# Attention output divided by its weight sums before it is turned, with values and sums in one stretch

## The chip, the cores and the metric

The kernel runs on one core of a Trainium2 chip. A core has a matrix engine (TensorE, PE in the profile; its weight loads are shown as PEld), a vector engine (VectorE, DVE), a scalar engine (ScalarE, ACT), a general engine (GpSimd, POOL) and a queue for transfers (SyncE, SP). Each engine works through its own list of instructions in the order of the program and waits where a semaphore of another engine is not there yet. Matmuls write to PSUM, which VectorE and ScalarE can read[...].

The metric is the device time of one execution in microseconds (us), smaller being better. Three runs of the kernel before took 3242.97, 3245.24 and 3245.39 us, so the median is 3245.24 us.

## The reference, cut to what matters

There are 32 batches (B) of 224 rows (S) with 512 features (D), and a context of 750 rows with 384 features per batch. Attention has 16 heads of 32 features. A head's output is the weighted sum of the values divided by the sum of the weights, which is what `softmax` followed by the product with `v` means:

```
attn = jnp.einsum('bhnd,bhmd->bhnm', q * scale, k)
attn = jnp.where(pad_mask[:, None, :, None], attn, jnp.float32(-1000000000.0))
attn = jax.nn.softmax(attn, axis=-1)
out  = jnp.einsum('bhnm,bhmd->bhnd', attn, v)
...
x = x + jnp.tanh(g_xattn[0]) * _L0_xattn_ref(_layernorm(x, axis=-1), ctx_768, ...)
x = x + jnp.tanh(g_ffn[0]) * _L0_ffn_ref(_layernorm(x, axis=-1), ...)
```

The second line of `x` is a feed-forward layer (512 to 2048 to 512) with quantised weights and activations, over all 7168 rows. The gate of the attention is multiplied into the value weights once at the start.

## The kernel before, in words

**Steps.** The attention is cut into 128 steps, one for each batch `b` and group `g` of four heads (128 features). A main loop (line 802) runs over the steps. The heads of a step share the 128 partitions of the matrix array, 32 rows or 32 columns each.

**What a step does.** The scores are computed twice. `maxima` (line 276) computes them with queries on the partitions (tile `sm`) in three parts, and VectorE takes the largest of each row (`mx`, 2.24 us a part). `minus_max` turns the maximum into three bfloat16 parts. `weights` (line 333) computes the scores again with context rows on the partitions (tile `se`), the maximum subtracted by an extra matmul from `nT`, and ScalarE takes `Exp` into the tile `p`, in three parts `u`. GpSimd adds the parts up into `acc`, which holds for each query the weights still to be summed over 125 partitions. `values` (line 366) multiplies the weights with the values into the PSUM tile `po`, features on the partitions and queries along the row. `sums` (line 380) multiplies `acc` with ones into the second half of the same tile, so that each feature's row has its weight sum beside it, and ScalarE copies both halves to the tile `oT`. `finish` (line 392) turns both halves with four transposes into `pyt`, queries on the partitions; VectorE takes the reciprocal of one column per head (`rd`), multiplies (`yo`), and GpSimd adds `yo` into `x`. After the fourth group of a batch the rows of `x` are stored to memory, from where the feed-forward layer loads them.

**Slots.** Step n of the main loop has six slots, 0 to 5. The even slots hold one part of `maxima` for step n+1, the odd slots one part of `weights` for step n. All of these use the one tile of the pool `ps_s` (four banks of PSUM, one buffer). So `sm`, its reduction on VectorE, `se`, its `Exp` on ScalarE and the next `sm` take turns, and TensorE has time between them for other matmuls, which I call the **cover** of the slot: in an even slot it covers the reduction, in an odd slot the `Exp`.

**What the covers are.** They are put in by hand with `put(slot, us, function)`. For step n−1 (called `last`), `values` goes to slot 1, `sums` to slot 3 and `finish` to slot 4. For later steps there are the keys (`pk`, one half in slot 0 and the other in slot 2), the queries (`pq`), the values (`pv`) and the turning of the normalised `x` (`pxn`). The turning of the maximum (`pn`) is in slot 0. Units marked `first=True` come directly behind the scores of the slot, then pieces of the feed-forward layer, then the other units:

```
            used = sum(us for us, _ in slots[k])
            early = [unit for us, unit in slots[k] if unit in quick]
            for unit in early:
                unit()
            ...
                ffn.fill(
                    (PE_ROOM[k % 2] - used, (1.1, 2.2)[k % 2], 1.7),
                    B if n == N and k > 4 else (n - 1) // NG if n else 0,
                )
```

**The planner.** `ffn.fill` takes pieces of the feed-forward layer (`ph`, `po` from `w2q`, the transposes `phq` and `pxq`, and their VectorE, ScalarE and GpSimd work) as long as they fit a room of microseconds per engine. The room of TensorE is 2.7 us in even and 2.2 us in odd slots, less what the units of the slot say they use. The numbers in `put` therefore move pieces between slots. While the weights of the feed-forward layer are being quantised (the first twelve steps) there are no such pieces. What is left when the steps are done follows behind them.

**Buffers.** The small PSUM tiles (`po`, `pyt`, `pk`, `pq`, `pv`, `ph` and so on) share the four buffers of the pool `ps_m`. Each engine's instructions keep the order in which the program issues them.

Of the kernel before, what the change touches and what calls it, by code (L numbers as in the profile page):

```python
# [8 lines left out]
F32 = mybir.dt.float32  # L9
# [5 lines left out]
ALU = mybir.AluOpType  # L15
# [9 lines left out]
def flamingo_gated_layer(  # L25
# [27 lines left out]
    pe, dve, act = Ordered(nc.tensor), Ordered(nc.vector), Ordered(nc.scalar)  # L53
    gp = Ordered(nc.gpsimd)
    P = 128
    B, S, D = x.shape
# [3 lines left out]
    NQ = 2  # L60
    CP = S // NQ
    H, DH = 16, 32
    HG = P // DH
# [13 lines left out]
    ident = const.tile([P, P], F32, name="ident")  # L77
# [53 lines left out]
    def pool(name, bufs, space=None):  # L131
        kw = {} if space is None else {"space": space}
        return es.enter_context(tc.tile_pool(name=name, bufs=bufs, **kw))
# [10 lines left out]
    smp = pool("small", 2)  # L144
# [6 lines left out]
    ps_m = pool("ps_m", 4, PSUM)  # L151
# [12 lines left out]
    x_of, y_of, q_of, k_of, v_of = {}, {}, {}, {}, {}  # L164
# [4 lines left out]
    def load_y(b):  # L169
        y_of[b] = yp.tile([P, NYC, M], F32, tag="y", name=f"y_{b}")  # L170
        nc.sync.dma_start(y_of[b], ctxT[b].rearrange("(c p) m -> p c m", p=P))

    def load_x(b):
        x_of[b] = xp.tile([CP, NQ, D], F32, tag="x", name=f"x_{b}")
        nc.sync.dma_start(x_of[b], x[b].rearrange("(t p) d -> p t d", p=CP))
# [52 lines left out]
    def k_units(b, g):  # L228
        kT = kp.tile([P, M], F32, tag="kT", name=f"kT_{b}_{g}")
        k_of[b, g] = kT  # L230

        def piece(half):
            pk = ps_m.tile([P, 512], F32, tag="m", name=f"pk_{b}_{g}_{half}")
            for c in range(NYC):
                pe.matmul(
                    pk[:, :MH], wkv_sb[:, c, g * P : (g + 1) * P],
                    y_of[b][:, c, half * MH : (half + 1) * MH],
                    start=(c == 0), stop=(c == NYC - 1),
                )
            act.copy(kT[:, half * MH : (half + 1) * MH], pk[:, :MH])  # L240

        return [lambda h=h: piece(h) for h in range(2)]
# [79 lines left out]
    def turn_max(n):  # L322
        b, g = steps[n]
        pn = ps_m.tile([P, NQ, CP], BF16, tag="m", name=f"pn_{b}_{g}")
        for t in range(NQ):
            pe.transpose(
                pn[:, t, :], nbs[n % 2][:, t].rearrange("p j r -> p (j r)"), identb[:CP, :CP]
            )
        nT = smp.tile([P, S], BF16, tag="nT", name=f"nT_{b}_{g}")
        act.copy(nT, pn.rearrange("p t n -> p (t n)"))  # L330
        nT_of[b, g] = nT
# [34 lines left out]
    def values(b, g):  # L366

        po = ps_m.tile([P, 512], F32, tag="m", name=f"po_{b}_{g}")
        po_of[b, g] = po
        v = v_of[b, g // 2]  # L370
        for c in range(NKC):
            for j in range(HG):
                at = ((g % 2) * HG + j) * DH
                pe.matmul(
                    po[j * DH : (j + 1) * DH, :S], v[:, c, at : at + DH],
                    p_of[b, g, c // 2][:, j, c % 2, :],
                    start=(c == 0), stop=(c == NKC - 1),
                )

    def sums(b, g):  # L380

        po, acc = po_of[b, g], acc_of.pop((b, g))
        for j in range(HG):
            pe.matmul(
                po[j * DH : (j + 1) * DH, S : 2 * S], ones[:KC, :DH], acc[:, j, :],
                start=True, stop=True,
            )
        oT = smp.tile([P, 2 * S], F32, tag="oT", name=f"oT_{b}_{g}")
        act.copy(oT, po[:, : 2 * S])
        po_of[b, g] = oT  # L390

    def finish(b, g):

        oT = po_of.pop((b, g))
        pyt = ps_m.tile([P, 2, NQ, P], F32, tag="m", name=f"pyt_{b}_{g}")
        for a in range(2):
            for t in range(NQ):
                at = a * S + t * CP
                pe.transpose(pyt[:CP, a, t, :], oT[:, at : at + CP], ident)
        rd = smp.tile([CP, NQ, HG], F32, tag="rd", name=f"rd_{b}_{g}")  # L400
        dve.reciprocal(
            rd, pyt[:CP, 1].rearrange("p t (j d) -> p t j d", j=HG)[:, :, :, 0]
        )
        yo = smp.tile([CP, NQ, P], F32, tag="yo", name=f"yo_{b}_{g}")
        dve.tensor_tensor(
            yo.rearrange("p t (j d) -> p t j d", j=HG),
            pyt[:CP, 0].rearrange("p t (j d) -> p t j d", j=HG),
            rd.unsqueeze(3).to_broadcast([CP, NQ, HG, DH]),
            ALU.mult,
        )  # L410
        cols = slice(g * P, (g + 1) * P)
        gp.tensor_tensor(x_of[b][:, :, cols], x_of[b][:, :, cols], yo, ALU.add)
        if g == NG - 1:
            nc.sync.dma_start(
                x1_d[b * S : (b + 1) * S, :].rearrange("(t p) d -> p t d", p=CP), x_of[b]
            )
# [361 lines left out]
    ks = k_units(0, 0) + k_units(0, 1)  # L778
# [23 lines left out]
    for n in range(N + 1):  # L802
        b, g = steps[n] if n < N else (B, 0)
        nxt = steps[n + 1] if n + 1 < N else None
        last = steps[n - 1] if 0 < n else None
        slots = [[] for _ in range(6)]
        quick = []

        def put(k, us, fn, first=False):
            slots[k].append((us, fn))  # L810
            if first:
                quick.append(fn)

        if n < N:
            put(0, 0.2, lambda: turn_max(n), first=True)
        if last:
            put(1, 2.3, lambda: values(*last), first=True)
            put(3, 0.5, lambda: sums(*last), first=True)
            put(4, 0.5, lambda: finish(*last), first=True)
        if n + 2 < N:  # L820
            ks = k_units(*steps[n + 2])
            put(0, 1.9, ks[0])
            put(2, 1.9, ks[1])
        if n < N and g == 2 and b + 2 < B:
            put(0, 0.0, lambda: (load_y(b + 2), load_x(b + 2)))
        more = b + 1 < B and n < N
        if more and g == 0:
            norm, turns, qs = q_units(b + 1)
            put(0, 0.0, norm[0], first=True)
            put(2, 0.0, norm[1], first=True)  # L830
            put(4, 0.0, norm[2], first=True)
            put(5, 2.7, lambda: v_piece(b + 1, 0, 0))
        if n < N and g < 2:
            put(3, 1.4, lambda: v_piece(b, 1, g + 1, 0))
            put(4, 1.4, lambda: v_piece(b, 1, g + 1, 1))
        if more and g == 1:
            put(0, 0.25, turns[0])
            put(2, 0.25, turns[1])
            put(5, 2.7, lambda: v_piece(b + 1, 0, 1))
        if more and g == 2:  # L840
            put(3, 1.5, qs[0])
            put(4, 1.5, qs[1])
            put(5, 2.7, lambda: v_piece(b + 1, 0, 2))
        if more and g == 3:
            put(3, 1.5, qs[2])
            put(4, 1.5, qs[3])
            put(5, 2.7, lambda: v_piece(b + 1, 1, 0))
        for k in range(6):
            if k % 2 == 0:
                if nxt:  # L850
                    maxima(*nxt, k // 2)
            elif n < N:
                weights(b, g, k // 2)
            if k == 4 and nxt:
                minus_max(n + 1)
# [5 lines that stand above are left out]
            if wunits:  # L861
                if k in (1, 3, 5):
                    wunits.pop(0)()
            else:
# [4 lines that stand above are left out]
            for us, unit in slots[k]:  # L869
                if unit not in quick:  # L870
                    unit()
# [39 lines left out]
```

## Time and profile before

| | us | instructions |
|---|---|---|
| median of three runs | 3245.24 | |
| profiled execution | 3241.06 | |
| its span | 3239.3 | 65769 |
| TensorE busy (matmuls) | 3060.1 | 28642 |
| VectorE busy | 1712.6 | 2501 |
| ScalarE busy | 1647.5 | 1803 |
| GpSimd busy | 2069.2 | 3048 |
| four transposes per step `pyt` | 83.5 | 512 |
| copy `oT` on ScalarE | 67.5 | 128 |
| `rd` and `yo` on VectorE | 25.3 and 54.3 | 128 and 128 |
| addition into `x` on GpSimd | 100.6 | 128 |

The span reaches from the first to the last instruction of the program, and 1.8 us of the profiled execution lie outside of it. The busy time of matmuls is longer than what they occupy, because their ends are modelled and they overlap; the distance from the start of one group of matmuls to the start of the next is what a group costs. Nearly all instructions are recorded by a helper and so have the line 51; they are told apart by the tiles they write and read. A step takes 25.3 us on average (3239.3 divided by 128).

### The profile page before, as it was taken

Reading aid. Unit: us, or ns where it says so; the run is one execution under the profiler, and the core shown is the slowest. Engines: PE = TensorE matmul, PEld = TensorE weight load, DVE = VectorE, ACT = ScalarE, POOL = GpSimd, SP = SyncE. Lnnn points to the kernel's source line nnn. Section 1 sums busy time; section 2 is a strip of 40 time slices with the busy share of each in tenths; the row PEclk is TensorE's granted clock in tenths of the full one; section 3 lists DMA queues with packets and bytes.
Section 4 is the critical chain, followed back from the end, with each engine's and each line's share of the span. In section 5 each row is a group of like instructions: output and inputs, shape, how many; then the busy total and the mean of one; then the engine's idle time right before and its main releaser. Section 6 shows DMA issues by size and latency. Waiting matters only on the chain. (4 is left out here: it accounts for less than half of the span.)

```text
span 3239.3 us, 65769 instructions
## 1 busy us (share of the span) xinstructions
PE 3060.1 (94%) x28642; PEld 1976.6 (61%) x28642; DVE 1712.6 (53%) x2501; ACT 1647.5 (51%) x1803; POOL 2069.2 (64%) x3048
## 2 busy tenths in 40 slices
PE   7989999999999999999999999999999999999975
PEld 5655566666666666666666666666666666666643
DVE  4576555554465455555554554555555545545533
ACT  2333555555555455455555554555455455555554
POOL 2565667666666676667666666765676666667664
PEclk9999999999999999999999999999999999999988
DMA  3322111010101001101000111001100011110000
GB/s 134 103 75 65 33 40 40 16 39 26 40 30 36 26 25 33 37 32 40 20 29 30 40 36 39 27 16 40 40 30 26 26 33 37 36 40 20 4 20 29
DMA packets 52817, 120.51 MB, mean 37 GB/s; under 512 B 3888, under 2 KB 3888, under 8 KB 52400
## 3 DMA queue, kind: packets, MB, share of 16 engines
q1 hardware_dynamic: 52528, 116.32, 11.0%
q8 instruction: 223, 3.65, 0.5%
q14 instruction: 66, 0.54, 0.1%
HBM read 86.94 MB, written 29.36 MB: 36 GB/s over the span
## 5 line engine op out<-in xcount | busy, mean ns | idle before, releaser
L51 POOL TENSOR_TENSOR acc<-acc,p 125x896 f32<-125x896 f32 x512 | 1069.4, 2089 | 518.3 <-ACT p L51 497.4
L51 DVE TENSOR_REDUCE mx<-sm 112x4 f32<-112x2000 f32 (+1 forms) x384 | 860.9, 2242 | 986.6 <-PE sm L51 986.6
L51 ACT ACTIVATE p<-se 125x1792 f32<-125x1792 f32 x384 | 638.8, 1664 | 413.1 <-PE se L51 407.1
L51 PE MATMUL pk<-y,wkv_sb 128*128 128x375 f32 x1536 | 537.8, 486 | 15.8 <-DMA wkv_sb<-in_wkvT 12.1
L51 PE MATMUL sm<-kT,qT 32*112 32x500 f32 (+1 forms) x4096 | 426.8, 508 | 35.2 <-ACT p L51 34.7
L51 POOL TENSOR_TENSOR acc<-p 125x896 f32<-125x896 f32 x128 | 267.3, 2089 | 273.0 <-ACT p L51 272.9
L51 ACT COPY kT<-pk 128x375 f32<-128x375 f32 x256 | 120.8, 472 | 581.9 <-PE pk L51 581.3
L51 PEld LDWEIGHTS pk<-y,wkv_sb 128*128 128x128 f32 x1536 | 278.6, 190 | 172.2 <-issue 26.7
L51 PE MATMUL pv_None<-wkv_sb,y 128*125 128x256 f32 x1536 | 364.1, 387 | 0.0
L51 PE MATMUL se<-qT,kT 32*125 32x224 f32 x6144 | 362.7, 349 | 0.0
L51 PE MATMUL po<-p,v 125*32 125x224 f32 x6144 | 321.4, 358 | 0.1
L51 PEld LDWEIGHTS pv_None<-wkv_sb,y 128*125 128x125 f32 x1536 | 278.4, 187 | 69.8 <-issue 33.4
L51 PEld LDWEIGHTS se<-qT,kT 32*125 32x125 f32 x6144 | 297.8, 183 | 0.0
L51 DVE SCALAR_TENSOR_TENSOR h<-ph,qa_am,b_sb 128x512 f32<-128x512 f32 x224 | 163.5, 744 | 197.2 <-PE ph L51 196.1
L51 PEld LDWEIGHTS sm<-kT,qT 32*112 32x112 f32 x4096 | 159.2, 170 | 166.8 <-issue 94.4
L51 PEld LDWEIGHTS po<-p,v 125*32 125x32 f32 x6144 | 188.1, 111 | 115.1 <-issue 40.1
L51 PE MATMUL ph<-w1q,xT 128*128 128x512 fp8e4 x896 | 226.8, 385 | 26.2 <-ACT xT L51 24.0
L51 PE MATMUL po<-w2q,hT 128*128 128x256 fp8e4 x1792 | 221.3, 279 | 13.1 <-DVE xg L51 7.1
L51 PE MATMUL pq<-xnT,wq_sb 128*128 128x224 f32 x1024 | 218.2, 356 | 0.2 <-ACT xnT L51 0.2
L51 PE MATMUL se<-nT,ones 3*125 3x448 bf16 x1536 | 157.2, 396 | 54.2 <-DVE mx L51 45.4
L51 POOL TENSOR_TENSOR x<-x,yo 112x256 f32<-112x256 f32 x128 | 100.6, 786 | 165.3 <-DVE yo L51 135.4
L51 PEld LDWEIGHTS <-hT 128*128 128x128 bf16 x1792 | 174.5, 100 | 48.3 <-issue 17.9
(102 smaller groups left out, 3497.3 us busy)
## 6 DMA issues: line engine op xcount, KB each, us to landing
y<-in_ctxT SPq DMA_DIRECT2D x32, 1125.0 KB, 5.4
x<-in_x SPq DMA_DIRECT2D x32, 448.0 KB, 3.9
x_d<-x SPq DMA_DIRECT2D x32, 448.0 KB, 3.1
xg<-x_d SPq DMA_DIRECT2D x28, 512.0 KB, 3.7
out<-xg SPq DMA_DIRECT2D x56, 256.0 KB, 2.1
wa<-in_w1T SPq DMA_DIRECT2D x8, 512.0 KB, 4.5
wa<-in_w2T SPq DMA_DIRECT2D x8, 512.0 KB, 4.0
wb<-in_w1T SPq DMA_DIRECT2D x8, 512.0 KB, 3.8
```

Source lines behind the costliest of these rows:

```text
L51: return lambda *args, **kw: tc.keep_in_program_order(build(*args, **kw))
```

## The change

The division moves to where the features lie on the partitions. `sums` no longer copies both halves of `po`. VectorE takes the reciprocal of the whole second half (128 partitions by 224) and multiplies it with the first half, both read from PSUM, into `oT`. `finish` turns one half only, with two transposes instead of four, and VectorE adds the result from PSUM into `x`. The copy on ScalarE, the small reciprocal, the multiplication `yo` and the addition on GpSimd are gone.

In the main loop `values` and `sums` stand one behind the other in slot 2, and the second half of the keys goes from slot 2 to slot 1. The units state 2.6 us and 0.3 us of TensorE instead of 2.3, 0.5 and 0.5 us, so the rooms of the planner change in slots 1 to 4.

```diff
-        oT = smp.tile([P, 2 * S], F32, tag="oT", name=f"oT_{b}_{g}")
-        act.copy(oT, po[:, : 2 * S])
+
+        oT = smp.tile([P, 2, S], F32, tag="oT", name=f"oT_{b}_{g}")
+        dve.reciprocal(oT[:, 1, :], po[:, S : 2 * S])
+        dve.tensor_tensor(oT[:, 0, :], po[:, :S], oT[:, 1, :], ALU.mult)
         po_of[b, g] = oT
 
     def finish(b, g):
 
         oT = po_of.pop((b, g))
-        pyt = ps_m.tile([P, 2, NQ, P], F32, tag="m", name=f"pyt_{b}_{g}")
-        for a in range(2):
-            for t in range(NQ):
-                at = a * S + t * CP
-                pe.transpose(pyt[:CP, a, t, :], oT[:, at : at + CP], ident)
-        rd = smp.tile([CP, NQ, HG], F32, tag="rd", name=f"rd_{b}_{g}")
-        dve.reciprocal(
-            rd, pyt[:CP, 1].rearrange("p t (j d) -> p t j d", j=HG)[:, :, :, 0]
-        )
-        yo = smp.tile([CP, NQ, P], F32, tag="yo", name=f"yo_{b}_{g}")
-        dve.tensor_tensor(
-            yo.rearrange("p t (j d) -> p t j d", j=HG),
-            pyt[:CP, 0].rearrange("p t (j d) -> p t j d", j=HG),
-            rd.unsqueeze(3).to_broadcast([CP, NQ, HG, DH]),
-            ALU.mult,
-        )
+        pyt = ps_m.tile([P, NQ, P], F32, tag="m", name=f"pyt_{b}_{g}")
+        for t in range(NQ):
+            pe.transpose(pyt[:CP, t, :], oT[:, 0, t * CP : (t + 1) * CP], ident)
         cols = slice(g * P, (g + 1) * P)
-        gp.tensor_tensor(x_of[b][:, :, cols], x_of[b][:, :, cols], yo, ALU.add)
+        dve.tensor_tensor(x_of[b][:, :, cols], pyt[:CP], x_of[b][:, :, cols], ALU.add)
...
         if last:
-            put(1, 2.3, lambda: values(*last), first=True)
-            put(3, 0.5, lambda: sums(*last), first=True)
-            put(4, 0.5, lambda: finish(*last), first=True)
+            put(2, 2.6, lambda: (values(*last), sums(*last)), first=True)
+            put(4, 0.3, lambda: finish(*last), first=True)
         if n + 2 < N:
             ks = k_units(*steps[n + 2])
             put(0, 1.9, ks[0])
-            put(2, 1.9, ks[1])
+            put(1, 1.9, ks[1])
```

## Prediction

> **What bounds the kernel now.** I read the page's busy times, the waits, then the timeline of one step.
>
> ```profile
> PE 3060.1 (94%) x28642; PEld 1976.6 (61%) x28642; DVE 1712.6 (53%) x2501; ACT 1647.5 (51%) x1803; POOL 2069.2 (64%) x3048
> ```
>
> TensorE is the bound: no other engine is over 64%. So an edit is worth what it takes from TensorE's list, or adds to its standstills. The waits name two of these:
>
> ```profile
> PEld sm L51 <- ACT p L51: 59.4, 63, 2.1
> ...
> PEld L51 <- DVE mx L51: 53.6, 58, 5.1
> ...
> PE se L51 <- DVE mx L51: 45.4, 120, 4.9
> ```
>
> Scores `se` wait for the reduction `mx`, scores `sm` for the `Exp` into `p`. The timeline of step 59 shows slots 2 to 4 (start, duration, engine, what, idle before):
>
> ```profile
> 1467.45 1.11 PE L51 MATMUL sm<-kT,qT 32*112 32x250 f32 x16
> ...
> 1468.49 2.16 PE L51 MATMUL pk<-y,wkv_sb 128*128 128x375 f32 x6
> ...
> 1470.92 0.41 PE L51 MATMUL se<-nT,ones 3*125 3x448 bf16 x4 [0.27 <-DVE mx L51]
> ...
> 1472.02 0.16 PEld L51 LDWEIGHTS po<-acc,ones 125*32 125x32 f32 x8 [0.28 <-issue]
> 1472.02 0.58 PE L51 MATMUL po<-acc,ones 125*32 125x224 f32 x8
> 1472.20 1.28 ACT L51 ACT_TABLE_LOAD   x1 [1.04 <-PE se L51]
> ...
> 1472.54 1.78 PE L51 MATMUL pq<-xnT,wq_sb 128*128 128x224 f32 x8
> ...
> 1475.21 1.11 PE L51 MATMUL sm<-kT,qT 32*112 32x500 f32 x8 [0.89 <-ACT p L51]
> ...
> 1476.25 0.65 PE L51 MATMUL pyt<-ident,oT 128*112 128x128 f32 x4
> ...
> 1476.74 1.68 PE L51 MATMUL pq<-xnT,wq_sb 128*128 128x224 f32 x8
> ...
> 1478.68 0.41 PE L51 MATMUL se<-nT,ones 3*125 3x448 bf16 x4 [0.27 <-DVE mx L51]
> ```
>
> Three things are to be seen. First, starts give each group's cost: `sums` 0.52 us, four transposes 0.49. From undisturbed places in the same way: half of the keys 1.98, `values` 2.41, `pq` 1.61, half a `pv` piece 1.39, `ph` 0.87, `phq` 0.45, a w2 piece 1.75. Second, from the end of `sm` to `se` an even slot takes 2.43 us however little stands between (1468.49 to 1470.92; 1476.25 to 1478.68): keys alone (1.98) lack 0.45, transposes and `pq` (2.09) lack 0.34. Third, the odd slots: from `se`'s start to `sm` with nothing between takes 2.72, of which `se` is 0.86, so the cover needed is 1.86, and about 1.92 typically. Behind a Gelu the table for `Exp` is loaded first (1.28) and 3.22 is needed; here 2.12 of cover lacks 1.1.
>
> **The Trainium skill.** "TensorEngine Tiling (Array Packing)", Key Properties, says that changing the tiling mode drains the engine. The trace agrees: every exit from the 32-wide tiles shows 0.28 of idle before the next load. "ScalarE: Activation LUTs", What ACT_TABLE_LOAD costs, gives about 1283 ns, as the trace has. "VectorE: DVE Perf Modes", tier table, puts fp32 `tensor_tensor` with a PSUM operand at one element per cycle; `yo` agrees (256 columns, 425 ns).
>
> **The change, part by part.**
>
> *Two transposes less.* The four start 0.11 apart after the first, so 2 × 0.109 = 0.22 us a step, × 128 = 27.9 us less on TensorE.
>
> *Sums behind values.* Both use 32-column tiles, so one drain goes. In `values` eight matmuls take 0.19; `sums` are two such rounds, 0.38 instead of 0.52. 0.137 × 128 = 17.5 us less. Together 45.4 us.
>
> *The covers.* I listed, from TensorE's order in both programs, what stands in each even and odd slot, and summed what it lacks against 2.43, 1.92 or 3.22:
>
> | slot | before | us | after | us |
> |---|---|---|---|---|
> | 0 | 49 × 0.34 (pn, keys) | 16.7 | 48 × 0.34 | 16.3 |
> | 1 | 17 loads × 0.81 (values) | 13.8 | 22 loads × 1.24 (keys), 3 × 0.79 | 29.7 |
> | 2 | 30 × 0.45 (keys) | 13.5 | none (values and sums 2.79) | 0 |
> | 3 | 15 loads, 0.65 to 1.31; 10 × 0.01 | 14.7 | 19 × 0.31 (pq), 13 × 0.53 (pv), 8 loads × 1.61, 2 × 0.08 | 25.9 |
> | 4 | 33 × 0.34, 11 × 0.55, 3 × 0.10 | 17.6 | 37 × 0.56, 26 × 0.77, 1 × 0.32 | 41.1 |
> | 5 | 17 loads × 0.44 | 7.5 | 17 × 0.44 | 7.5 |
> | last two steps | | 12.7 | | 14.4 |
> | sum | | 96.5 | | 134.9 |
>
> So 38.4 us of standstill are added. Half of the transposes' gain is lost where it arises, because slot 4 is short of cover already; `sums` leave slot 3 bare; only slot 2 gains. The check on before: beyond each group's shortest distance to the next, TensorE stands still 148 us up to step 125. My list explains 96, and 28 are 21 places where `ph` stands right behind `pxq` and waits for the copy to `xT` (1.27 and more each). Some 24 are left, mostly in the second step of a batch, where VectorE is late with `xn`.
>
> *The pieces shift.* The planner's new order has 15 such `pxq`–`ph` places: 6 × 1.27 = 7.6 us less. Behind the last step both orders have the same 34 groups.
>
> *VectorE.* It loses `rd` (0.20) and `yo` (0.43) and gains a product of 224 columns (`yo`'s row less 32 columns, 0.39), an addition of 256 (0.43) and a reciprocal of 128x224, which the trace doesn't show. From below: one column per cycle, 0.39. From above: the same VectorE page says, in its walkthrough of the pipeline, that the division repeats eight times; at eight cycles of 0.96 GHz per column, an estimate, 1.87 + 0.16 = 2.0. `rd` (8 columns, 198 ns against 156 for one) speaks for the lower part; I take 0.39. It hardly matters. Queued behind the two new instructions are slot 2's and 3's evictions (`h`, `xg`, `v`), `hm`, and then `mx` of slot 4, for which TensorE waits. From the end of `sums` to the end of slot 4's scores at least 3.85 us pass; VectorE's list there comes to 2.1 on average and 3.45 at most. With 2.0 for the reciprocal some six steps overflow, 2 us in all. If that cover went, each microsecond would cost 128.
>
> *ScalarE and GpSimd.* The copy `oT` (0.53) and the addition (0.79, and its waits for `yo`, 135 us) go. Neither engine is the bound: nothing, beyond an earlier `acc`. No transfer is added; the store of `x` is issued behind VectorE's addition instead of GpSimd's.
>
> *A new wait.* `sums` wait for `acc`, now in the middle of slot 2. Placing them there in the trace of before, `acc` was done at least 1.2 us earlier in all steps, 7.7 in the median. GpSimd has less to do after the change: nothing. Everything on TensorE is queued behind this wait.
>
> *The end.* In the last step `values` fall behind two w2 pieces, on the way to the last store of `x`; about 2.8 later, and 0.9 earlier by the hop over GpSimd and a hidden copy: 1 us more, an estimate.
>
> Sum: −45.4 + 38.4 − 7.6 + 1 = −13.6. On the span 3239.3 − 13.6 = 3225.7, as an execution 3241.06 − 13.6 = 3227.5. The profiled execution is 4.2 below the median of the runs, so I predict 3245.2 − 13.6 = 3231.6, rounded 3232.
>
> **Rivals.**
>
> *The gain is eaten.* The 24 unexplained microseconds grow to 38 or so, since VectorE gets more to do just before the late steps and evictions that free `ps_m` come later. For it: waits of TensorE for VectorE up to 5.1. Against: behind slot 4's `mx` VectorE's list is shorter than before (3.8 against 4.1 on average). It ends near 3245.
>
> *The gain stays whole.* GpSimd, freed of the addition, has the scales for `xn` ready earlier, so that most of the 24 go, and `po` holds a buffer for one slot instead of three. Then 3232 − 20 = 3212. For it: VectorE waited for GpSimd's `ve`, up to 4.1. Against: only three such waits.
>
> *Slower: `sums` wait for `acc`.* Place: slot 2, with nothing else to do on TensorE. In seven steps only 1.2 to 2 us were in hand, where the feed-forward layer puts up to 7 us of small work between the parts of `acc`, and the planner moves this work. The sign turns when these waits exceed 13.6 us, a result slower than noise at 20: each of the 28 pairs of row tiles would have to stop TensorE for 0.7. At 1.5 each, 42 us, it ends at 3274. Against: the longest lists between parts of `acc` are no longer than before.
>
> *It does not do what it says:* the order shows the two transposes gone and the groups adjacent in every step, so no.
>
> **How the numbers follow.** Forecast (6.5 to 22 us faster) 0.45, whole gain 0.17, eaten 0.21, slower 0.17. 0.2% or 6.5 us is about what a measurement can tell from no change. So faster 0.62, same 0.21, slower 0.17. The forecast's own range is 3223 to 3239. The range 3204 to 3256 takes in the eaten gain, the whole one with both terms' errors, and the smaller half of the waits for `acc`.
>
> **What would show it.** Right: `pyt` with 256 matmuls and some 28 us less between starts; 0.38 from `sums` to the next group less the drain; slot 4 short by 0.56 and 0.77 in about 63 steps; no wait before `se` in slot 2; waits of `sm` for `p` up by some 30 us in slots 1 and 3; VectorE busier by about 0.6 a step. Wrong: a wait of `po<-acc` for `acc`; reductions `mx` that start late after slot 4's scores; a reciprocal above 2 us; or a standstill of TensorE in slots that the table calls covered.

## The result, and the profile after

The changed kernel takes 3220.02 us (median of four runs, 3218.53 to 3220.15) beside 3245.31 us of the kernel before (four runs too). The ratio is 0.9922, with a 95% interval of 0.9909 to 0.9934. That is 25.3 us less, where the prediction had 13.6 less. The profiled execution took 3220.14 us with a span of 3218.4, which is 20.9 less than the span before.

The page of the changed kernel, busy times:

```profile
PE 3027.6 (94%) x28386; PEld 1958.6 (61%) x28386; DVE 1919.8 (60%) x2629; ACT 1580.8 (49%) x1675; POOL 1974.1 (61%) x2920
```

TensorE is the bound as before. VectorE has 207 us more to do. The groups of instructions (busy us, mean ns of one, then the idle time ahead of it) show of what:

```profile
L51 DVE RECIPROCAL oT<-po 128x224 f32<-128x224 f32 x128 | 199.3, 1557 | 76.2 <-PE po L51 76.2
L51 PE MATMUL pyt<-ident,oT 128*112 128x128 f32 x256 | 55.6, 299 | 2.2 <-DVE oT L51 2.2
L51 DVE TENSOR_TENSOR x<-pyt,x 112x256 f32<-112x256 f32 x128 | 53.0, 414 | 0.0
L51 DVE TENSOR_TENSOR oT<-po,oT 128x224 f32<-128x224 f32 x128 | 50.1, 391 | 4.4
```

The product and the addition have the forecast durations (0.39 and 0.41 against 0.39 and 0.43). The reciprocal takes 1.56 us, four times the 0.39 that I used, within the bounds of 0.39 and 2.0. The waits that answer to the three shown before:

```profile
PEld sm L51 <- ACT p L51: 115.7, 138, 3.5
...
PE se L51 <- DVE mx L51: 62.1, 115, 2.9
PEld L51 <- DVE mx L51: 51.4, 69, 1.7
```

Scores `sm` wait for `Exp` 56 us longer. By the slots, some 29 of these are in slots where ScalarE loads its table first, and most of the rest in slots 1 and 3 without a load, which lost `values` and `sums` as their cover. The waits for `mx` are up from 99.0 to 113.5 in total, but the longest fell from 5.1 to 2.9. (Each line has the total in us, the number and the longest.) No wait of `po<-acc` for `acc` is left in the list at all. Step 58 (counted from 0, one step earlier than the one in the prediction), slots 2 to 4, in the timeline of the changed kernel:

```profile
1449.85 1.11 PE L51 MATMUL sm<-kT,qT 32*112 32x250 f32 x16 [1.07 <-ACT p L51]
1450.89 2.48 PE L51 MATMUL po<-p,v 125*32 125x224 f32 x48
1453.19 0.56 PE L51 MATMUL po<-acc,ones 125*32 125x224 f32 x8
...
1454.65 0.41 PE L51 MATMUL se<-nT,ones 3*125 3x448 bf16 x4
...
1458.23 1.11 PE L51 MATMUL sm<-kT,qT 32*112 32x500 f32 x8
1459.27 0.43 PE L51 MATMUL pyt<-ident,oT 128*112 128x128 f32 x2
1459.54 1.03 PE L51 MATMUL ph<-w1q,xT 128*128 128x512 fp8e4 x4
...
1462.01 0.41 PE L51 MATMUL se<-nT,ones 3*125 3x448 bf16 x4
```

Slot 2 holds values and sums, and `se` no longer waits there. From the start of the values to the start of the sums 2.30 us pass; values and sums alone cost 2.41 and 0.52 before, and the two together now cost 2.79 (1450.89 to 1453.68, the start of the piece `ph` behind them). Two transposes take 0.27 to the next start, where four took 0.48. Both terms of TensorE's gain are as forecast.

**Where the time went.** I cut each span at the first `pn` of steps 16 and 126. The first stretch holds the twelve steps in which the weights of the feed-forward layer are prepared; from step 126 on the attention runs out. The table also has all experiments (0 is the changed kernel):

| | kernel | median, us | to step 16 | 16 to 126 | from 126 |
|---|---|---|---|---|---|
| – | before | 3245.3 | 401.7 | 2702.4 | 135.2 |
| 0 | changed | 3220.0 | 410.3 | 2679.6 | 128.4 |
| 1 | new division, old slots | 3243.7 | 427.4 | 2682.2 | 132.2 |
| 2 | old division, new slots | 3226.3 | 405.4 | 2694.2 | 124.6 |
| 3 | copy in place of the reciprocal | 3209.0 | 397.7 | 2679.5 | 126.1 |
| 4 | two reciprocals | 3239.5 | 425.3 | 2684.7 | 130.1 |
| 5 | four transposes | 3228.0 | 406.6 | 2691.7 | 126.9 |
| 6 | no quantising in slot 3 | 3207.8 | 395.9 | 2680.4 | 128.8 |
| 7 | before, new places in the last step | 3257.3 | 403.8 | 2706.3 | 147.7 |
| 8 | last step: attention first | 3221.2 | 408.0 | 2680.1 | 131.3 |
| 9 | pieces to the short slots | 3232.5 | 397.9 | 2678.9 | 154.9 |
| 10 | sums alone in slot 3 | 3283.5 | 427.6 | 2695.2 | 158.4 |
| 11 | old places from step 126 on | 3220.5 | 408.0 | 2680.3 | 132.9 |

Stretches of one profile scatter. Experiment 7 has the program of before up to the last step and is at step 126 6.0 us later; 8 and 11 have that of the changed kernel and are there 1.7 us earlier. So differences of a few microseconds in a stretch say little. The kernel before was run again beside each experiment, with medians of 3244.6 to 3245.8 us, so medians from different times can be compared to about 1 us.

The changed kernel loses 8.6 us up to step 16, gains 22.8 in the main part and gains 6.8 at the end. The prediction's sum runs over all steps alike and has +1 for the end: it had no loss for the first stretch and no gain for the last.

### The profile page after: what moved, and what is told of

Read it like the earlier page. It is cut to its first block, busy times and chain, and to the rows that moved or that the text cites. A ratio compares the mean times of both kernels' runs of the same rounds, so it can differ in the third digit from the quotient of the medians.

```text
span 3218.4 us, 65118 instructions
## 1 busy us (share of the span) xinstructions
PE 3027.6 (94%) x28386; PEld 1958.6 (61%) x28386; DVE 1919.8 (60%) x2629; ACT 1580.8 (49%) x1675; POOL 1974.1 (61%) x2920
## 5 line engine op out<-in xcount | busy, mean ns | idle before, releaser
L51 PE MATMUL pk<-y,wkv_sb 128*128 128x375 f32 x1536 | 542.2, 489 | 13.5 <-DMA wkv_sb<-in_wkvT 12.3
L51 PEld LDWEIGHTS sm<-kT,qT 32*112 32x112 f32 x4096 | 159.6, 171 | 213.2 <-ACT p L51 115.7
L51 DVE RECIPROCAL oT<-po 128x224 f32<-128x224 f32 x128 | 199.3, 1557 | 76.2 <-PE po L51 76.2
L51 PE MATMUL se<-nT,ones 3*125 3x448 bf16 x1536 | 157.4, 397 | 66.8 <-DVE mx L51 62.1
```

What stands on the lines that cost most here:

```text
L51: return lambda *args, **kw: tc.keep_in_program_order(build(*args, **kw))
```

## The experiments

### 1 and 2: each half of the change alone

Experiment 1 has the first hunks of the change (division, two transposes, addition on VectorE) and the old `put` lines with their old numbers. Experiment 2 has the old division and the new `put` lines:

```diff
-            put(1, 2.3, lambda: values(*last), first=True)
-            put(3, 0.5, lambda: sums(*last), first=True)
-            put(4, 0.5, lambda: finish(*last), first=True)
+            put(2, 2.6, lambda: (values(*last), sums(*last)), first=True)
+            put(4, 0.3, lambda: finish(*last), first=True)
...
-            put(2, 1.9, ks[1])
+            put(1, 1.9, ks[1])
```

> The division of the changed kernel in the slots and with the stated microseconds of the kernel before (values in slot 1, sums in slot 3), so that TensorE's order is that of before less two transposes a step. Theory A, the account of TensorE's groups and covers: 27.9 us less for the transposes, 10.4 us more lack of cover in slot 4, so 17.5 us faster than before (3228), if the reciprocal of 1.56 us stays hidden. It may not here: from the end of sums in slot 3 to the end of slot 4's scores there are only some 2.4 us in the steps without feed-forward pieces, and the two new instructions take 1.95; every 0.1 us that the reduction starts late costs up to 12.8 us. Theory B, the freed GpSimd and ScalarE made the gain and not TensorE's list: then this kernel, which frees them in the same way, has the whole 25 us (3220).

> Values and sums in slot 2 and the second half of the keys in slot 1 with the stated microseconds of the changed kernel, but the division of before (copy on ScalarE, four transposes, small reciprocal, product, addition on GpSimd). TensorE's order is that of the changed kernel with two transposes more. Theory A: 17.5 us less for the joined groups, 24.3 us more lack of cover, 7.6 us less for places of ph behind pxq: 0.8 us faster than before, no difference that can be measured. Theory B: no difference either, since no engine is freed, but then the late second steps of the batches stay as before. What tells: whether slot 0's standstill (53 us before, 32 after) falls here too, by the order, or not, by the freed engines.

Measured: the division alone 3243.7 us, ratio 0.9996 (0.9987 to 1.0004), so no difference; the slots alone 3226.3 us, ratio 0.9939 (0.9927 to 0.9952). Both expectations missed: the first had 3228 or 3220 us, the second no difference.

What follows: the division alone gains 20.2 us in the main part and gives it all back up to step 16, where it is 25.7 us slower. By the starts and the standstills of TensorE, the 20.2 us are 24 for the transposes, less 9 for slot 4's missing cover, and 5 from slot 0, which no term of the prediction has. The slots alone gain 8.2 in the main part and 10.6 at the end, and lose 3.7 up to step 16. The halves help each other: with both, the loss up to step 16 is 8.6 instead of 25.7. The reason is the reciprocal's place. In the old slots it follows the sums in slot 3, directly ahead of slot 4's reduction; in the new ones it comes a slot earlier. Experiment 10 tests this: with the sums alone moved back to slot 3, the changed kernel takes 427.6 us up to step 16, as here (427.4).

### 3 and 4: what the reciprocal costs

```diff
-        dve.reciprocal(oT[:, 1, :], po[:, S : 2 * S])
+        dve.tensor_copy(oT[:, 1, :], po[:, S : 2 * S])
```

Experiment 3 leaves the division out: the values are multiplied with the sums. Experiment 4 computes the reciprocal a second time into a tile that nobody reads.

> The changed kernel with a plain copy of the weight sums in place of the reciprocal: the division is left out (the values are multiplied by the sums), so VectorE does 128 copies of some 0.39 us instead of 128 reciprocals of 1.56 us, 150 us less work. Theory A, the reciprocal is hidden behind slot 3: the steps from the seventeenth on keep their time within 5 us; only the first sixteen steps, where VectorE also quantises the weights and which took 8.6 us longer than before, win back up to 9 us. So 0 to 12 us faster than the changed kernel. Rival: the reciprocal is partly exposed by late reductions in slot 4 (58 us of standstill there): 20 to 40 us faster.

> The changed kernel with the reciprocal taken twice (the second into a spare tile that nobody reads), 1.56 us more of VectorE in every step, right behind the first and ahead of the product. Theory A: the time from the end of sums to the end of slot 4's scores is at least 3.85 us and the list of VectorE there now comes to 3.2 us on average; 1.56 more makes it 4.8, so about half of the steps overflow, by 0.5 to 1 us each: 30 to 70 us slower than the changed kernel. If VectorE had no weight at all: no difference. If it were the bound: 200 us slower.

Measured: 3209.0 us (ratio 0.9893, 0.9878 to 0.9908) and 3239.5 us (0.9986, 0.9980 to 0.9993). The copy takes 391 ns in the profile, so 1.17 us of VectorE go in each of 128 steps, 149 us in all; the second reciprocal adds 1.50 us a step, 191 us in all. The medians move by 11 us down and 19 us up from the changed kernel; the first was expected (0 to 12 us), the second is less than the 30 to 70 us expected.

What follows: in the main part the reciprocal costs nothing (2679.5 against 2679.6), and a second one costs 5.1 us. Nearly everything is paid up to step 16: 12.6 us for the one, 15.0 more for the other. The argument that the reciprocal hides behind slots 2 and 3 holds where the feed-forward layer runs, and fails while its weights are quantised.

### 5: how much of the two transposes was kept

The second half of `oT` is turned too, into a `pyt` of four parts, and not read:

```diff
             pe.transpose(pyt[:CP, t, :], oT[:, 0, t * CP : (t + 1) * CP], ident)
+            pe.transpose(pyt[:CP, NQ + t, :], oT[:, 1, t * CP : (t + 1) * CP], ident)
```

> The changed kernel, with the second half of oT (the reciprocals) turned too, as before the change: two more transposes in slot 4 of every step, whose result nobody reads. The theory of covers: they cost 0.22 us in each of 128 steps, 27.9 us of TensorE's list, but slot 4 lacks 0.56 to 0.77 us of cover in some 66 of 127 steps, where they fill a standstill; so about half is seen, +14 us, 3234 us. The rival, that work on TensorE is worth its duration wherever it stands: +28 us, 3248 us. A second rival, that slot 4 waits for VectorE in nearly every step: under +5 us, 3225 us at most.

Measured: 3228.0 us, 8.0 more than the changed kernel, where 14 were expected; ratio to before 0.9948 (0.9936 to 0.9961). In the main part it is 12.1 us later, where the two transposes cost 110 × 0.218 = 24.0 us by their starts. So one half was seen there, as the list of covers says; the other half fills standstills that slot 4 has anyway. Up to step 16 it is not later but 3.7 us earlier, with more work for TensorE. The next experiment and the clock explain how that can be.

### 6: the quantising units away from slot 3

While the weights are prepared, one unit per odd slot is put on VectorE: sixteen sums of magnitudes first (1.2 us each), and from step 6 to step 11 sixteen quantising units of three instructions each. In experiment 6 the quantising units stand in slots 1 and 5 only:

```diff
-                if k in (1, 3, 5):
+                if k in (1, 5) or (k == 3 and len(wunits) > 16):
                     wunits.pop(0)()
```

> The changed kernel, with the sixteen quantising units of the weights (about 2.2 us of VectorE each, up to 6 where GpSimd is busy) in slots 1 and 5 alone and no longer in slot 3, where the reciprocal now stands in VectorE's list; the stage gets about three steps longer. If the 8.6 us that the changed kernel loses up to step 16 are the reciprocal and such a unit together ahead of slot 4's reduction, 5 to 9 us come back up to step 16, and up to 3 are lost by the later start of the feed-forward pieces: 3215 us. The rival, that this loss comes from where keys and values now stand on TensorE: no gain, 3220 to 3224 us.

Measured: 3207.8 us (3206.98 to 3208.63), ratio 0.9884 (0.9870 to 0.9897). That is the fastest of all kernels here, 12.2 us faster than the changed one, where 5 were expected. Up to step 16 it is 14.4 us earlier, and in the other stretches it is within 0.8 us. About half of the 14.4 us is work that moved: the changed kernel runs eight `ph` pieces and one `pxq`, 7.4 us by their starts, before step 16, and this kernel runs them in its main part, which takes no longer for it. So the units in slot 3 made the loss, and nothing is lost by the later start of the feed-forward layer. Experiment 3, without the division but with these pieces in their old place, comes to the same time (3209.0).

How the loss arises is seen in one step of the changed kernel, in the timeline of the stage:

```profile
207.41 1.56 DVE L51 RECIPROCAL oT<-po 128x224 f32<-128x224 f32 x1 [0.54 <-PE po L51]
209.00 0.39 DVE L51 TENSOR_TENSOR oT<-po,oT 128x224 f32<-128x224 f32 x1
209.31 0.74 DVE L51 TENSOR_SCALAR wb<-wb,wscale 128x1024 f32<-128x1024 f32 x1
210.08 0.69 DVE L51 TENSOR_SCALAR wb<-wb 128x1024 f32<-128x1024 f32 x1
210.81 2.45 DVE L51 TENSOR_SCALAR w1q<-wb 128x1024 fp8e4<-128x1024 f32 x1
213.18 2.23 DVE L51 TENSOR_REDUCE mx<-sm 112x4 f32<-112x2000 f32 x1
...
210.38 4.81 POOL L51 TENSOR_TENSOR acc<-acc,p 125x896 f32<-125x896 f32 x2 [4.97 <-ACT p L51]
...
210.29 1.11 PE L51 MATMUL sm<-kT,qT 32*112 32x500 f32 x8
...
215.47 0.64 PE L51 MATMUL se<-nT,ones 3*125 3x448 bf16 x4 [2.19 <-DVE mx L51]
215.79 1.81 PE L51 MATMUL se<-qT,kT 32*125 32x224 f32 x16
217.53 5.15 PE L51 MATMUL pv_None<-wkv_sb,y 128*125 128x256 f32 x12
222.61 1.11 PE L51 MATMUL sm<-kT,qT 32*112 32x500 f32 x8
```

Reciprocal, product and three quantising instructions follow each other without a gap from 207.41 to 213.2. Slot 4's scores start at 210.29 and are done about 1.04 later, by the distance to the next group, but their reduction starts at 213.18. TensorE stands still for 2.19 us. And then its matmuls take longer: `pv_None` 5.15 us. The third quantising instruction takes 2.45 us instead of 0.69: GpSimd had begun an addition into `acc` at 210.38. In the thirteen traces 120 of these instructions took over 1 us; every one of them overlapped a GpSimd addition and ended 0.55 us after that addition. In experiment 6 the same slots read:

```profile
204.84 1.54 DVE L51 RECIPROCAL oT<-po 128x224 f32<-128x224 f32 x1
...
209.15 2.24 DVE L51 TENSOR_REDUCE mx<-sm 112x4 f32<-112x2000 f32 x1 [2.35 <-PE sm L51]
...
211.44 0.41 PE L51 MATMUL se<-nT,ones 3*125 3x448 bf16 x4 [0.49 <-DVE mx L51]
...
212.54 2.85 PE L51 MATMUL pv_None<-wkv_sb,y 128*125 128x256 f32 x12
215.32 1.11 PE L51 MATMUL sm<-kT,qT 32*112 32x500 f32 x8
```

Now VectorE waits for the scores. From `se` to the next `sm` 3.88 us pass (211.44 to 215.32) instead of 7.14 (215.47 to 222.61). So this one standstill of 2.19 us cost another 3.3 us behind it. The granted clock of TensorE shows how. Five windows of the changed kernel (start and end, length, then the busy times of PE, PEld, DVE, ACT and POOL with their instructions, then the granted clock, the DMA share and GB/s):

```profile
208.57:211.99 3.42, 3.28 (x21) 2.18 (x21) 3.32 (x5) 1.96 (x2) 1.61 (x1) 1.00 0.00 0
211.99:215.40 3.41, 1.28 (x7) 1.06 (x6) 3.41 (x2) 0.34 (x1) 3.12 (x2) 1.00 0.28 86
215.40:218.81 3.41, 3.34 (x23) 2.60 (x23) 3.14 (x11) 1.06 (x1) 0.00 (x0) 0.50 0.20 74
218.81:222.23 3.42, 3.42 (x9) 2.65 (x9) 0.32 (x1) 0.60 (x1) 2.60 (x2) 0.50 0.47 153
222.23:225.64 3.41, 3.41 (x18) 1.45 (x17) 1.86 (x1) 0.93 (x2) 1.55 (x1) 1.00 0.00 0
```

In the window with the standstill TensorE is busy for 1.28 of 3.41 us. In the next two it is busy again, but the clock is 0.50. In all thirteen traces the granted clock is either 1.00 or 0.50 and changes only at the edges of windows of 3.41 us. Cut along these windows from 40 us on, all traces agree: at full clock, no window with less than 1.6 us of standstill was followed by half clock, and each one with 2.0 us or more was; between the two both occur. There are 154 such falls. In experiment 5, whose two extra transposes shorten the same standstill, TensorE is busy for 1.52 us of that window, and the clock stays at 1.00.

Up to step 16 half clock lasts 20.5 us in the changed kernel, 3.4 in the kernel before and in experiment 3, 10.2 in experiments 5 and 6, 34.1 in experiment 1 and 41.0 in experiment 10. At half clock at most half of the time is lost, so as an estimate up to 8.5 of the 8.6 us that the changed kernel loses there are clock. No kernel that changes the clock and nothing else was run, so the chain from standstill to clock is read from these traces, not isolated.

### 7, 8 and 11: the end

The old and new places of the attention's last units, in different steps:

```diff
 # 7: the kernel before
-            put(1, 2.3, lambda: values(*last), first=True)
-            put(3, 0.5, lambda: sums(*last), first=True)
+            put(1 if n < N else 2, 2.3, lambda: values(*last), first=True)
+            put(3 if n < N else 2, 0.5, lambda: sums(*last), first=True)
 # 8: the changed kernel
-            put(2, 2.6, lambda: (values(*last), sums(*last)), first=True)
-            put(4, 0.3, lambda: finish(*last), first=True)
+            put(2 if n < N else 0, 2.6, lambda: (values(*last), sums(*last)), first=True)
+            put(4 if n < N else 1, 0.3, lambda: finish(*last), first=True)
 # 11: the changed kernel
+            if n > N - 3:
+                put(1, 2.3, lambda: values(*last), first=True)
+                put(3, 0.5, lambda: sums(*last), first=True)
+            else:
+                put(2, 2.6, lambda: (values(*last), sums(*last)), first=True)
```

> The kernel before, with the new slots in the last step alone (values and sums both in slot 2, behind the feed-forward pieces of slots 0 and 1); 126 of the 128 steps are as they were. If the gain behind step 126 in the kernel with the new slots (10.6 us) comes from the last step, where values, sums and transposes each stood behind pieces and behind a wait for a rounded row: -7 us, 3238 us. The rival, that the gain comes from an earlier progress of the feed-forward layer through the planner: no difference, 3245 us. What the prediction had for the end: +1 us, 3246 us.

> The changed kernel, with values and sums in slot 0 of the last step and the transposes in slot 1, ahead of the feed-forward pieces that stand in slots 0 to 3 there. The pieces (two turns and four w2 pieces, some 9 us with their waits) then lie behind the last transposes, where TensorE stands still for 18 us and waits for the last rows to come back from memory. Expected: -7 us, 3213 us. The rival: sums then wait for the last parts of acc on GpSimd, so that only 2 to 3 us are won, 3217 us.

> The changed kernel, with the old places in the last three turns of the loop alone (values in slot 1, sums in slot 3, from step 126 on); all before it is as changed, and behind the last transposes TensorE has the same groups. From the start of step 126 to the end the changed kernel takes 128.4 us and the kernel before 135.2. If the places of values and sums in these last steps make the difference: +7 us, 3227 us, and the stretch from step 126 takes 135 us. The rival, that it comes from what the planner had already put off or done when step 126 begins: no difference, 3220 us and 128 to 129 us.

Measured: experiment 7 3257.3 us, ratio 1.0037 (1.0025 to 1.0050); experiment 8 3221.2 us, 0.9919 (0.9906 to 0.9933); experiment 11 3220.5 us, 0.9925 (0.9911 to 0.9938). Experiments 7 and 8 missed every number that was expected. In experiment 11 the time is the rival's, while the stretch from step 126 in its profile, 132.9 us, lies between the two. The profiles tell more. First the last full step, from its `pn` to its last transposes, as a window of the kernel before, of the changed kernel and of experiment 11, in this order:

```profile
3124.63:3160.84 36.21, 24.82 (x278) 16.86 (x275) 5.66 (x10) 19.78 (x18) 27.38 (x50) 0.76 0.02 9
```

```profile
3111.99:3140.62 28.63, 20.87 (x276) 15.54 (x273) 6.38 (x11) 15.42 (x13) 21.41 (x28) 0.86 0.05 20
```

```profile
3110.38:3145.45 35.07, 25.47 (x275) 17.69 (x273) 7.55 (x11) 15.64 (x13) 21.37 (x30) 0.74 0.04 16
```

With the new places this takes 28.6 us, with the old ones 35.1, and before the change it took 36.2. So 6.4 of the 7.6 us that the changed kernel gains here come with the places of values and sums. They are not waits alone: the granted clock is 0.86 with the new places and 0.74 to 0.76 with the old ones, so half clock lasts some 8 us instead of 17 to 18, and up to 5 us of the 6.4 are clock, an estimate by the same rule. But the whole of experiment 11 is only 0.4 us slower than the changed kernel: what is behind the last transposes takes 2.0 less there, and this step began 1.6 earlier, which leaves 2.8 in the span of its profiled execution, the slowest of its five. How much of the 6.4 reaches the end is therefore open.

Experiment 7 does not gain in that stretch (36.4 from `pn` to the last transposes): the wait of `phq` for the rounded row, 3.2 us behind the values before, now stands ahead of them with 6.0. It loses 12 us behind the last transposes: from there to the end it takes 90.8 us instead of 78.5, where the planner's last pieces stand in another order and the granted clock is 0.73 instead of 0.80. In experiment 8 the sums wait for the last parts of `acc` on GpSimd, as its rival had it, here in its timeline:

```profile
3134.68 0.59 PE L51 MATMUL po<-acc,ones 125*32 125x224 f32 x8 [3.29 <-POOL acc L51]
```

The transposes come only 0.8 us earlier by that, and, counted from them, the last pair of rows comes 3.9 us later. So the standstill behind the last transposes was no free room for the pieces; the likely reason, not tried apart, is that their work on the other engines now stands in the lists ahead of the last rows.

### 9: pieces moved to the slots that lack cover

Experiment 6 with rooms by slot:

```diff
-                    (PE_ROOM[k % 2] - used, (1.1, 2.2)[k % 2], 1.7),
+                    ((1.5, -9, 0.5, 0.9, 1.2, -9)[k], (1.1, 2.2)[k % 2], 1.7),
...
+            if name.startswith("gelu") and self.k not in (3, 5) and not self.end:
+                return False
```

> The kernel of the sixth experiment (no quantising unit in slot 3), and the planner's TensorE room per slot set by cover instead of by even and odd: 1.5 us for slot 0, none for slot 1 (but what late rows add to slot 0), 0.5, 0.9 and 1.2 for slots 2, 3 and 4, none for slot 5; a Gelu is put only in slots 3 and 5, and late rows weigh 0.15 instead of 0.3 from four row tiles on. By the list of TensorE's order the lack of cover falls from 139 to 109 us and the places where ph stands right behind pxq from 13 to 5 (about 11 us less); behind the last step 42 groups are left instead of 34, 7 us more. The theory of covers: 3207.8 - 30 - 11 + 7 = 3174 us. The rival, that where pieces go matters little because the engines behind them (ScalarE and VectorE, which the new order may collide with) set the slots: 3200 us or more.

Measured: 3232.5 us, ratio 0.9960 (0.9946 to 0.9974), 25 us slower than experiment 6 and not 34 faster. The main part is 1.5 us shorter, which is no gain, since some 12 us of pieces have moved out of it. The end is 26 us longer, with 42 groups of pieces behind the last transposes instead of 34; 12 of the 26 are those pieces themselves, and the rest was not taken apart. Up to step 125 slot 4 stands still for 36 us instead of 48, as intended, but slot 0 for 48 instead of 33 and slot 1 for 42 instead of 34. The list of covers had promised 30 us less in all. It knows TensorE's order only; where pieces move, the work of the other engines moves too, and waits arise that the list has no term for, such as three of `pxn` for ScalarE's `v`, 13.7 us together.

### 10: sums by themselves in slot 3

```diff
-            put(2, 2.6, lambda: (values(*last), sums(*last)), first=True)
+            put(2, 2.3, lambda: values(*last), first=True)
+            put(3, 0.5, lambda: sums(*last), first=True)
```

> The changed kernel, with the sums by themselves in slot 3 and the values alone in slot 2. TensorE pays one more drain in each step, 17.5 us by the starts. By the list of TensorE's order the lack of cover falls from 135 to 118 us (slot 3 gets 0.52 of cover; table loads move from slot 1 to slot 5), and a place of ph behind pxq is added (1.3 us). Covers and starts alone: 3220 + 17.5 - 16.5 + 1.3 = 3222 us, so that joining the sums to the values brings next to nothing here. The rival, that VectorE counts too: the reciprocal now stands in VectorE's list right ahead of the reduction of slot 4's scores, for which TensorE waits; with 0.5 us or more in each step that is 3280 us and above. If joined sums were worth their 17.5 us on top of all else: 3237 us.

Measured: 3283.5 us, ratio 1.0118 (1.0104 to 1.0132), 63.5 us slower than the changed kernel. The rival that VectorE counts is right, and the waits of this kernel show it:

```profile
PE se L51 <- DVE mx L51: 102.3, 136, 5.6
```

It was 62.1, with 2.9 at most. Slot 4 stands still for 104 us instead of 58. By stretches, 17.3 us are lost up to step 16, 15.6 in the main part, and 30.0 at the end, where 42 groups of pieces are left instead of 34. So the place of the sums is worth more by what it does to VectorE's list than by the drain that it saves, and half of the loss lies at the end, with a backlog of pieces that this edit happened to cause.

## Why the prediction was right and where it was wrong

The direction, and the time within the range, were right; the forecast was 12 us too slow. 12 is 7.8 for the end, 4.2 for the profiled execution of before, which was that much under its median while the changed kernel's was not (3220.14 beside 3220.02), and what remains is under 1 us. Up to step 126 the forecast has −14.6 and the runs −14.2, but that agreement is luck in part: the first stretch lost 8.6 us for which there was no term, and slot 0 gained what no term has. The pieces of the sum:

- **TensorE's groups, −45.4.** Right. The starts show 2.79 for values and sums together, forecast 2.41 + 0.52 − 0.14 = 2.79, and 0.27 for two transposes, forecast 0.48 − 0.22 = 0.26. Experiment 5 gives half of the transposes back in the main part, as the table of covers says. Two readings beside these terms were wrong, without weight in the sum: in `values` four matmuls take 0.19, not eight; and 0.28 of idle stands behind `se`, but 0.36 behind values and sums and 0.33 or 0.75 behind `sm`, so not at every exit.
- **Covers, +38.4, and fewer `pxq`–`ph` places, −7.6.** Up to step 125 the standstills of TensorE (time less the groups' own durations) grow by 28.3 us, where these terms, without the last two steps' 1.7, give 29.1. By slot, measured and in brackets forecast: slot 0 −20.9 (−0.4), slot 1 +11.6 (+15.9), slot 2 −15.1 (−13.5), slot 3 +10.5 (+11.2), slot 4 +31.7 (+23.5), slot 5 +10.3 (0). The brackets have the covers alone; the fewer `pxq`–`ph` places lie mainly in slot 2 (six there before, none after). Slots 1 to 3 come near. Slot 0 and slots 4 and 5 are both wrong and cancel, so that the sum agrees is luck.
- **Slots 4 and 5.** The step that failed is "it hardly matters" under VectorE. The list of VectorE's work between the sums and slot 4's reduction, at most 3.45 us, was that of the feed-forward stage. In steps 6 to 11 a quantising unit of 2.1 us and more stands there as well, and with a reciprocal of 1.56 us instead of 0.39 the list overflows: slot 4 stands still for 2.0 to 3.0 us in steps 6, 7, 8 and 10, where it was 0.3 to 0.6 before. Slot 5 has a covered `Exp` in these steps; what it shows is `se` and `pv_None` at half clock. In the main part the step was right: experiment 3 changes it by 0.1 us. Experiment 6 takes the unit away, and slots 4 and 5 fall by 10.5 and 10.9 us, which is more than they had over the forecast.
- **Slot 0.** The rival of the whole gain said that most of the 24 unexplained microseconds, the late second steps, would go. That is what happened: places in slot 0 with more than 0.8 us of standstill fell from 18 (37.8 us) to 9 (14.4 us). Each half of the change alone does part of it (10 places with 22.5, 13 with 23.8). That GpSimd's freed time is the reason, as the rival had it, is not shown. In the main part it speaks against it that experiment 2, which leaves the addition on GpSimd, gains 13.1 of slot 0's 13.8 us, and experiment 1, which frees GpSimd, 4.9. Which part of the new order does it was not tried.
- **The end, +1.** Wrong, by far the largest error: −6.8. The prediction counted the two w2 pieces ahead of the values in the last step, and did not count that before the change sums and transposes stood behind the same pieces, with a wait for a rounded row between them, nor the step ahead of it, nor that standstills there lower the clock (0.76 before, 0.86 after). The same groups were to be walked through with their waits in both orders, as for a slot, and were not. Which of these makes the 6.8 us stays open: the new places in the last step alone gained nothing (experiment 7), and the old places at the end cost 0.4 us by the medians (experiment 11).
- **The waits of sums for `acc`** did not come: no such wait in the changed kernel.
- **The reciprocal.** The page "VectorE: DVE Perf Modes" of the Trainium skill, from whose walkthrough of the pipeline I had the upper bound of 2.0, was nearer than the 0.39 that I took from the small reciprocal `rd`; 1.56 was measured. I misread `rd`: 198 ns for 8 columns and 156 for one are 42 ns for seven columns, 6 a column, and 156 + 223 × 6 is 1494 ns.

## What to carry to other kernels

Check a hidden instruction's cover in every stage of the program, not only in the longest one: here six of 128 steps had a fuller VectorE and took back 8.6 us of a gain of 30, and moving their units brought 12. A list of TensorE's covers forecast one given reordering well, if partly because two errors cancelled, but as a guide for choosing a new order it failed by 58 (3232.5 instead of 3174), since pieces take their other engines' work with them. Walk through the last steps group by group with their waits, and look at how much is left behind the last step, because edits of the order moved that stretch by up to 30 us.

## What the runs showed of the hardware

- VectorE's reciprocal costs about 6.3 ns a column: 1557 ns for 224 columns beside 153 for one column, so (1557 − 153) / 223. A copy of the same 224 columns takes 391.
- A standstill of TensorE can cost more than its length. After 2.19 us without work the granted clock was 0.50 for two windows of 3.41 us, and the next groups took 1.81 instead of 0.98 and 5.15 instead of 2.85. In the thirteen traces 2.0 us of standstill within one such window were always followed by half clock, and less than 1.6 never. In the changed kernel four groups `pv_None` between 190 and 300 us took 3.7 to 5.2 us instead of 2.8, 6 us together; in the kernel before and in experiment 6 none did.
- One VectorE instruction of the quantising unit, 0.69 us in most places, takes 2.45 in some. All 120 instructions of these units that took over 1 us overlapped a GpSimd addition and ended 0.55 us after its end, as if they had waited for it.
